# Grouped FFNs with two sends in flight and a longer clear, softmax rows divided before they are turned, late routing split

## The chip, the cores and the metric

The kernel runs on one core of a Trainium2 chip. The metric is the device time of one execution in microseconds (us). A core has five engines with an instruction stream each: TensorE (PE in the profile; PEld is its weight loading), VectorE (DVE), ScalarE (ACT), GpSimd (POOL) and SyncE (SP), and DMA queues that move data between on-chip memory and the chip's main memory. SP's and POOL's instruction streams issue the transfers that matter here: SP plain ones, POOL the indirect ones, in which every partition of a tile goes to, or comes from, a row whose number stands in an index tile.

## The reference

The program is a "macaron" of two layers on x of 8 x 512 x 256 fp32, which are 4096 tokens of 256 columns:

```python
x = x + 0.5 * _L0_ffn_ref(_layernorm(x), ...)    # 8 experts that choose their tokens
x = x + _L0_attn_ref(_layernorm(x), ...)         # rope, causal, 16 heads of 16
x = x + 0.5 * _L0_ffn_ref(_layernorm(x), ...)
x = x + 0.5 * _L1_ffn_ref(_layernorm(x), ...)    # 16 experts, grouped routing, top 4
x = x + _L1_attn_ref(_layernorm(x), ...)         # 16 heads of 64, returns x + z
x = x + 0.5 * _L1_ffn_ref(_layernorm(x), ...)
```

The last three lines are those that the change touches. In the grouped FFN every token gets a softmax over 16 experts; the best two of four groups stay, and of their experts the best four are taken, with the softmax values as weights:

```python
g = scores.reshape(T, N_GROUPS, N_EXPERTS // N_GROUPS)
_, gidx = lax.top_k(g.max(axis=-1), TOPK_GROUPS)
...
masked = (g * gmask[..., None]).reshape(T, N_EXPERTS)
_, indices = lax.top_k(masked, TOPK)
weights = jnp.take_along_axis(original_scores, indices, axis=1)
...
a = jax.nn.silu(h1) * h3
y = jnp.einsum('tei,eid,te->td', a, w2, c)
z = jax.nn.silu(xt @ ws1) * (xt @ ws3) @ ws2
return (y + z).reshape(shape)
```

Expert width is 128, the shared expert's 256. In the second attention

```python
scores = jnp.einsum('bhqk,bhmk->bhqm', q, k) * scale
weights = jax.nn.softmax(scores, axis=-1)
z = jnp.einsum('bhqm,bhmk->bhqk', weights, v)
```

with q, k and v from three projections of the normalized x, and z times `w_o` added to x.

## The kernel before

The 4096 tokens are 32 token tiles of 128 (TT = 32), four of them (QT = 4) to a sequence of 512 (CH). x stays in on-chip memory throughout. `tile_kernel` (L2392) runs `ffn0`, `attn0`, `ffn0`, then `ffn1_before` (L2149, the first grouped FFN, class `Grouped`), `attn1` (L1029) and `ffn1_after` (L2297, the last grouped FFN, class `Joint`, a subclass of `Grouped`). From L2149 on the order of the instructions on every engine is the one written in the code.

**A grouped FFN.** The tokens are cut into two parts (12 and 20 tiles in the first, `PARTS`; 20 and 12 in the last, `LAST`). For each part, `logits` on PE, then `routing` on DVE (with a few products on PE) gives every token four slot numbers, sorted by expert (`slot`), and four weights (`coef`). `send` (L1488, in `Joint` L1844 on) issues four indirect DMAs for each token tile on POOL, which write the tile's normalized rows to their slots in main memory (`slots_d`). A send waits until an earlier send has landed: in `Grouped` the one three before it (`self.sent[-3:-2]`, the third last of those issued), in `Joint` the one two before it. Behind the four sends `Grouped.send` lets POOL clear `self.pause`, 128 x 512. `tile_steps` then runs over the slots in steps of two tiles of 128 rows: SP loads `xs`, PE transposes (`turn`, `tpx`), multiplies by w1 and w3 of the tile's expert (`hide`, `hs`), transposes (`back`, `tpa`) and multiplies by w2 (`give`, `yps`); the stages of four successive steps are interleaved, and SP stores `ys` to `ys_d`. The loads of a part wait for all sends of the part. Evictions from PSUM go to ACT or DVE by the parity of the step (`evict`). Last, `gather` on POOL fetches the four rows of each token from `ys_d` into `yg`, with a clear behind each four, and `add` on DVE adds them, weighted, to x.

In `ffn1_before` the shared expert's products fill PE while the routing and the sends of part 0 run. The gathers of part 1 come in `attn1`, whose code also prepares part 0 of the last FFN: means and roots of the layer norm, normalized rows on POOL (L1484), transposes and logits (`Front`), its routing (`routing`, one piece at a time, from chunk NC * groups + 7 = 47 on) and its 80 sends. `ffn1_after` loads the expert weights on SP (for each group of four experts w1, w3 and w2, all 512 columns wide or less), runs the first three steps of part 0, normalizes the last four token tiles, computes their logits, routes all 12 tiles of part 1 on DVE while PE goes on with part 0, and sends them as soon as the slots are there. The gathers begin at step `known + 3`, and the rest of them is spread over the shared expert's units.

**The second attention.** A chunk is one sequence and two heads: 64 chunks (N), 8 (NC) to a sequence, each in two halves of two query tiles. The loop at L1281 goes through half-steps g. Half-step g holds: the turning of the first of the two query tiles of half-step g - 1 (`turn`: 4 transposes for each head into `tp`, evicted to `eT` by ACT for the first head, DVE for the second), a piece of side work (`pieces`), the projection to q (evicted by ACT) or k (by DVE) of the next chunk (`side`), the turning of the second query tile, the scores of this half-step (`scores`: 4 products into `sp`, DVE takes the negated maximum of each query tile, ACT the exponentials with their sums into `ex`), and a filling (`fill`) that PE does while DVE and ACT work: in half 0 the products of the weights with v of the chunk before (`products`, `zp`), in half 1 projections of the sequence before (`project`) or columns and values of the next.

The exponentials are turned as they are. The division by the row sums comes behind the products: `reciprocals` takes 1/sums of a chunk (DVE), and ACT spreads them to `wide`, 128 x 512; `spread` turns `wide` on PE (4 transposes into `rp`), ACT copies the result to `rs`; `scale` multiplies `zp` by `rs` on DVE into `zn`. All PSUM tiles named `tp`, `rp`, `pq`, `pv`, `yp`, `row` share one tag of three buffers ("m").

`roots` computes the layer norm's 1/sqrt in two pieces with a square root on ACT (`ln_root`) and Newton steps on DVE (`ln_rest`); `ln_guess` (L195) does the same on DVE alone, from integer operations and three Newton steps.

Of the kernel before, what the change touches and what calls it, by code (L numbers as in the profile page):

```python
# [19 lines left out]
P = 128  # L20
# [49 lines left out]
class Kernel:  # L70
# [124 lines left out]
    def ln_guess(self, pool, stats, t0, n):  # L195

# [11 lines left out]
        for i in range(3):  # L208
# [5 lines left out]
            y = new  # L214

# [820 lines left out]
    def _attn1(self, ctx, weights, one, after):  # L1036
# [61 lines left out]
        def scores(n, half):  # L1098
# [4 lines left out]
            sps = []  # L1103
# [9 lines left out]
            for i, sp in enumerate(sps):  # L1113
# [3 lines left out]
                ex = ch["ex", qt] = work.tile([P, 2, CH], F32, name="ex", bufs=4)  # L1117
                for j in range(2):
                    nc.scalar.activation(  # L1119
                        ex[:, j, :], sp[:, j, :], AF.Exp,  # L1120
                        bias=nmax[:, j : j + 1], accum_out=ch["sums"][:, qt, j : j + 1],
                    )

# [9 lines left out]
        def reciprocals(n):  # L1133
            ch = chunk[n]
            rec = work.tile([P, QT, 2], F32, name="rec", bufs=2)
            nc.vector.reciprocal(rec, ch["sums"])
            ch["wide"] = work.tile([P, QT, 2, DK1], F32, name="wide", bufs=1)
            nc.scalar.copy(ch["wide"], bc(rec, 3, DK1))

        def spread(n):  # L1140
            ch = chunk[n]
            rp = bank("rp")
            for qt in range(QT):
                nc.tensor.transpose(  # L1144
                    rp[:, qt * P : qt * P + P], ch["wide"][:, qt].rearrange("p h d -> p (h d)"), self.ident
                )
            ch["rs"] = work.tile([P, CH], F32, name="rs", bufs=1)
            nc.scalar.copy(ch["rs"], rp)
# [13 lines left out]
        def scale(n):  # L1162
            zn = work.tile([P, CH], F32, name="zn", bufs=11)
            nc.vector.tensor_tensor(zn, chunk[n]["zp"], chunk[n]["rs"], ALU.mult)
# [29 lines left out]
        def roots(ranges):  # L1194
            ys = []

            def first():
                for stats, t0, n in ranges:
                    ys.append(self.ln_root(pool, stats, t0, n))

            def second():
                for (stats, t0, n), y in zip(ranges, ys):
                    self.ln_rest(pool, stats, t0, n, y)
            return [first, second]
# [75 lines left out]
        side(0, 1)  # L1280
        for g in range(2 * N + 1):  # L1281
# [3 lines left out]
            if half == 0 and n < N:  # L1285
                todo += listed(n)
            if half == 1 and n > 0:
                scale(n - 1)
            if g > 0:
                turn(m, 2 * mh, 0)  # L1290
                turn(m, 2 * mh, 1)
            if half == 0 and n > 0:
                reciprocals(n - 1)
            pieces(1)
            if n + 1 < N:
                side(n + 1, half)
# [3 lines left out]
            if half == 0 and n > 0:  # L1300
                spread(n - 1)
            if n < N:
                scores(n, half)
# [8 lines left out]
                for piece in fill(n, half):  # L1312
                    piece()
            else:
                products(n - 1)
        scale(N - 1)
# [4 lines left out]
        for i in range(QT):  # L1321
            project(B - 1, i)
            self.ln_mean(self.late, after.stats, (B - 1) * QT + i)

# [137 lines left out]
class Grouped:  # L1462
# [25 lines left out]
    def send(self, h, t, row):  # L1488
# [3 lines left out]
        for r in range(TOPK):  # L1492
# [6 lines left out]
            before = self.sent[-3:-2]  # L1499
# [157 lines left out]
    def expert_weights(self, groups=range(4)):  # L1657
        nc, w = self.k.nc, self.k.w
        for g in groups:
            es = slice(g * 4, g * 4 + 4)  # L1660
            nc.sync.dma_start(
                out=self.w13[:, es, :, 0:INTER], in_=w["w1"][es].rearrange("e (c p) i -> p e c i", p=P)
            )
            nc.sync.dma_start(
                out=self.w13[:, es, :, INTER:], in_=w["w3"][es].rearrange("e (c p) i -> p e c i", p=P)
            )
            nc.sync.dma_start(out=self.w2[:, es], in_=w["w2"][es].rearrange("e p d -> p e d"))
# [821 lines left out]
```

## Time and profile before

| what | us |
|---|---|
| three runs, median (lowest to highest) | 3820.96 (3817.65 to 3825.62) |
| profiled execution, its time | 3822.71 |
| its span in the profile | 3821.0 |
| `ffn0`, `attn0`, `ffn0` | 0 to about 1741 |
| `ffn1_before` | 1741 to 2168 |
| `attn1`, with its last projections | 2168 to 3409 |
| `ffn1_after` | 3409 to 3821 |
| PE busy in 2168 to 3391 | 1212.0 of 1223 |
| DVE, ACT, POOL busy there | 749.2, 645.0, 240.0 |
| PE busy in 3409 to 3620 | 179.9 of 211 |
| PE busy in 3620 to 3821 | 170.7 of 201; POOL 151.4 |

The stages are told apart by the lines of their instructions. A group of the profile is one line of code, one engine and one form of operation, with its count, its busy time in us, the mean in ns of one, and behind the second bar the time that the engine stood idle just ahead of it and what it then waited for. An arrow in a timeline's brackets gives the idle time before an instruction and its releaser. The granted clock of PE over the span is 0.968 of full speed.

The two largest groups of the second attention show its shape:

```profile
L1119 ACT ACTIVATE ex<-sp,nmax 128x512 f32<-128x512 f32 x512 | 345.1, 686 | 238.8 <-DVE nmax L1116 238.7
...
L1116 DVE TENSOR_REDUCE nmax<-sp 128x2 f32<-128x1024 f32 x256 | 301.6, 1220 | 81.4 <-PE sp L1110 81.4
```

### The profile page before, as it was taken

How to read it: one execution, taken by the hardware profiler on the slowest of the kernel's cores; microseconds unless marked ns; L12 is line 12 of the kernel's file. 1: busy time of each engine (PE TensorE's matmuls, PEld its weight loads, DVE VectorE, ACT ScalarE, POOL GpSimd, SP SyncE). 2: the span in 40 equal slices, each digit the busy share in tenths (PEclk: the TensorE clock that was granted, in tenths of full speed). 3: DMA queues.
4: the chain of work that ended last, by engine and by line, in shares of the span. 5: the costliest groups of instructions: out<-in, count | busy, mean ns of one | idle time of the engine just before them, and what ended most of it. 6: DMA issues, size and time to landing. Idle time of an engine off the chain costs nothing.

```text
span 3821.0 us, 51805 instructions
## 1 busy us (share of the span) xinstructions
PE 3583.2 (94%) x18293; PEld 2235.2 (58%) x18293; DVE 1860.9 (49%) x4500; ACT 1451.8 (38%) x2922; POOL 1244.2 (33%) x1142
## 2 busy tenths in 40 slices
PE   4999999999996899998989999999999999988988
PEld 1566664555553566666678745555555555557865
DVE  6212205665655312116535566666556567546355
ACT  3222223444444222221123355555555555532321
POOL 2333235343331333333763312220000002714177
PEclk7999999999998899998999999999999999999989
DMA  5355442000113233324467401000000000135564
GB/s 194 97 139 146 109 103 85 23 18 23 29 34 96 49 69 78 71 41 134 135 219 236 135 18 31 28 26 1 1 1 1 1 1 23 72 113 185 163 182 130
DMA packets 258173, 309.32 MB, mean 81 GB/s; under 512 B 34048, under 2 KB 227968, under 8 KB 257664
## 3 DMA queue, kind: packets, MB, share of 16 engines
q1 hardware_dynamic: 182144, 177.78, 14.8%
q0 software_dynamic: 49152, 101.24, 10.7%
q10 hardware_dynamic: 26624, 27.00, 2.1%
q8 instruction: 151, 2.47, 0.3%
q14 instruction: 102, 0.84, 0.1%
HBM read 159.51 MB, written 138.02 MB: 78 GB/s over the span
## 4 chain that ended last, share of the span: by engine, by line
PE 37%; issue 8%; POOL 6%; DMA 2%; DVE 1%; ACT 0%; POOLq 0%; DVEq 0%; SPq 0%; ACTq 0%
PE sp L1110 6%; PE tp L1130 6%; PE pq L1088 6%; PE zp L1157 6%; PE pv L1077 3%; PE yp L1172 3%; POOL slots_d L1493 3%; PE hs L1786 2%; POOL yg L2010 2%; PE hs L2073 1%; PE yps L1808 1%; POOL slots_d L1857 1%; PE rp L1144 1%; DMA yg<-ys_d,slot 1%; PE yps L2095 1%
## 5 line engine op out<-in xcount | busy, mean ns | idle before, releaser
L521 PE MATMUL hp<-exT,w 128*128 128x512 f32 x1024 | 453.4, 597 | 0.7 <-DVE exT L509 0.7
L552 PE MATMUL op<-w,hid 128*128 128x256 f32 x2048 | 451.9, 379 | 0.0
L1119 ACT ACTIVATE ex<-sp,nmax 128x512 f32<-128x512 f32 x512 | 345.1, 686 | 238.8 <-DVE nmax L1116 238.7
L552 PEld LDWEIGHTS op<-w,hid 128*128 128x128 f32 x2048 | 386.8, 190 | 64.1 <-issue 14.4
L557 DVE TENSOR_TENSOR ob<-op,b 128x256 f32<-128x256 f32 x128 | 54.4, 425 | 642.8 <-PE op L552 555.3
L1116 DVE TENSOR_REDUCE nmax<-sp 128x2 f32<-128x1024 f32 x256 | 301.6, 1220 | 81.4 <-PE sp L1110 81.4
L531 POOL DMA_INDIRECT acc_d<-ob,idx x128 | 201.7, 1576 | 419.3 <-ACT ob L558 353.2
L812 DVE CUSTOM_DVE_ANT_0 junk<-sp,mask 128x128 bf16<-128x128 f32 (+3 forms) x512 | 251.2, 491 | 166.4 <-PE sp L803 142.3
L521 PEld LDWEIGHTS hp<-exT,w 128*128 128x128 f32 x1024 | 192.8, 191 | 221.5 <-issue 216.7
L1130 PEld LDWEIGHTS tp<-ident,ex 128*128 128x128 f32 x2048 | 233.8, 141 | 144.7 <-issue 84.7
L525 ACT ACTIVATE hid<-hp,b 128x512 f32<-128x512 f32 x256 | 175.9, 687 | 317.0 <-PE hp L521 317.0
L1130 PE MATMUL tp<-ident,ex 128*128 128x128 f32 x2048 | 272.9, 275 | 6.6 <-ACT ex L1119 4.1
L1110 PE MATMUL sp<-qk,qk 64*128 64x512 f32 x1024 | 254.4, 615 | 0.0
L1601 POOL DMA_INDIRECT yg<-ys_d,slot x128 | 129.6, 1013 | 359.2 <-DVE x L1614 267.0
L1088 PE MATMUL pq<-xnT,wide 128*128 128x512 f32 x512 | 244.1, 600 | 1.2 <-ACT xnT L250 0.8
L252 DVE COPY eT<-tp 128x512 f32<-128x512 f32 x256 | 177.1, 692 | 138.7 <-PE tp L1130 138.5
L1157 PE MATMUL zp<-eT,v 128*64 128x512 f32 x1024 | 234.0, 598 | 0.0
L250 ACT COPY eT<-tp 128x512 f32<-128x512 f32 x256 | 149.8, 585 | 220.1 <-PE tp L1130 220.1
L492 POOL DMA_INDIRECT ex<-xn_d,idx x128 | 131.5, 1027 | 297.8 <-DVE idx L483 263.6
L558 ACT ACTIVATE ob<-ob,gate 128x256 f32<-128x256 f32 x128 | 65.0, 508 | 413.9 <-DVE ob L557 413.9
L1059 POOL TENSOR_TENSOR x<-x,xn 128x1024 f32<-128x1024 f32 x8 | 18.9, 2360 | 544.1 <-DVE xn L1054 544.1
L855 ACT ACTIVATE ex<-st 128x1024 f32<-128x1024 f32 x160 | 155.1, 1022 | 95.1 <-PE st L848 95.1
(432 smaller groups left out, 6024.6 us busy)
## 6 DMA issues: line engine op xcount, KB each, us to landing
xs<-slots_d SPq DMA_DIRECT2D x149, 256.0 KB, 2.9
ys_d<-ys SPq DMA_DIRECT2D x149, 256.0 KB, 2.9
w<-in_W SPq DMA_DIRECT2D x32, 1024.0 KB, 5.2
slots_d<-zero ACTq DMA_DIRECT2D x7, 2304.0 KB, 12.8
w_sb<-in_w SPq DMA_DIRECT2D x24, 512.0 KB, 7.6
xn_d<-xn SPq DMA_DIRECT2D x16, 512.0 KB, 3.1
acc_d<-x SPq DMA_DIRECT2D x16, 512.0 KB, 4.4
x<-acc_d SPq DMA_DIRECT2D x16, 512.0 KB, 7.0
```

Source lines behind the costliest of these rows:

```text
L252: self.nc.vector.tensor_copy(out, in_)
L521: nc.tensor.matmul(hp, lhsT=w1[:, c, f * P : f * P + P], rhs=exT[e][:, c, h * CH : h * CH + CH], start=(c == 0), stop=(c == DC - 1),)
L525: nc.scalar.activation(hid[h][:, f, :], hp, AF.Gelu, bias=b1[:, e, f : f + 1])
L531: inst = nc.gpsimd.indirect_dma_start(out=acc_d[:, :], out_offset=bass.IndirectOffsetOnAxis(ap=idx[:, e, st : st + 1], axis=0), in_=ob, in ...
L552: nc.tensor.matmul(op, lhsT=hid[h][:, f, i * P : i * P + P], rhs=w2[:, f, :], start=(f == 0), stop=(f == FC - 1),)
L812: nc.vector.tensor_tensor_reduce(out=junk[:, :wd], in0=sps[h // 2][:, h % 2, at : at + wd], in1=mask[:, S - wd :], scale=1.0, scalar=NEG, ...
L1088: nc.tensor.matmul(pp, lhsT=(wq, wk)[a][:, k, c * P : c * P + P], rhs=xnT[b][:, k, :], start=(k == 0), stop=(k == DC - 1),)
L1110: nc.tensor.matmul(sp[:, j, :], lhsT=q[r, qt * P : qt * P + P], rhs=k[r, :], start=True, stop=True)
L1116: nc.vector.tensor_reduce(nmax, sp, AX.X, ALU.max, negate=True)
L1119: nc.scalar.activation(ex[:, j, :], sp[:, j, :], AF.Exp, bias=nmax[:, j : j + 1], accum_out=ch["sums"][:, qt, j : j + 1],)
L1130: nc.tensor.transpose(tp[:, k, :], ch["ex", qt][:, j, k * P : k * P + P], self.ident)
L1157: nc.tensor.matmul(zp[DK1 * j : DK1 * j + DK1, :], lhsT=v[b, h][:, k, at : at + DK1], rhs=ch["eT"][:, j, k, :], start=(k == 0), stop=(k == ...
```

## The change

**Sends of the first grouped FFN.** A send waits for the one two before it; the clear behind each four is 128 x 1024.

**The second attention.** `reciprocals` and `spread` are gone. `divide`, new, takes the reciprocals of one query tile's two sums on DVE and scales the two heads' exponentials in place before they are turned: on DVE, or, where `shared` holds, the first head on ACT. `shared` holds for chunks up to parts[1] + 2 = 22, in which the gathers and sums of the first FFN run, and from chunk 47 until part 0 of the last FFN is routed. The division of the first query tile stands behind its exponentials and ahead of the second's, that of the second behind the half-step's filling. `scale` becomes a copy on ACT. Where the filling of the half-step before was empty, `side` comes ahead of the first turning. `roots` uses `ln_guesses`, the pieces of `ln_guess`.

**Routing of the last FFN's second part.** `routing` is split: `choose` is what depends on a token tile alone (softmax, groups, top four). Two `choose` of four tiles each run in `attn1`, the first from half-step 2 * (N - NC) + 4 on as 13 pieces of two advances, the second behind the last half-step; what they find is kept in a `yg` buffer (`kept`). `ffn1_after` chooses for the last four tiles only and then goes on with all 12. `Cut` gives tiles of the full size and returns their first columns.

**Weights and order of the last FFN.** The host lays w1 and w3 together in the order of the on-chip tile, and w2 too. SP issues w13 of three groups, four loads of `xs`, w13 of the fourth group, w2 in two halves, the shared weights. Two steps, the root and the normalized rows, the third step, then columns and logits. `lean` sends the evictions of the steps to ACT while the routing runs. Two of the `normal`s move between the sends. In `Joint`, sends of part 1 have a clear of 1024 columns behind each four. The gathers start at `known + 5`, and in the shared part three half-tokens come to four units.

```diff
--- before.py
+++ after.py
...
-        def scores(n, half):
+        def scores(n, half, shared):
...
-            sps = []
+            sps, exps = [], []
...
+                exps.append((qt, sp, nmax, ex))
+            for qt, sp, nmax, ex in exps:
                 for j in range(2):
                     nc.scalar.activation(
                         ex[:, j, :], sp[:, j, :], AF.Exp,
                         bias=nmax[:, j : j + 1], accum_out=ch["sums"][:, qt, j : j + 1],
                     )
+                if qt == 2 * half:
+                    divide(n, qt, shared)
...
+        def divide(n, qt, shared):
             ch = chunk[n]
...
+            rec = work.tile([P, 2], F32, name="rec", bufs=4)
+            nc.vector.reciprocal(rec, ch["sums"][:, qt])
+            ex = ch["ex", qt]
+            for j in range(2):
+                if shared and j == 0:
+                    nc.scalar.mul(ex[:, j, :], ex[:, j, :], rec[:, j : j + 1])
+                else:
+                    nc.vector.tensor_scalar(ex[:, j, :], ex[:, j, :], rec[:, j : j + 1], None, ALU.mult)
...
-            nc.vector.tensor_tensor(zn, chunk[n]["zp"], chunk[n]["rs"], ALU.mult)
+            nc.scalar.copy(zn, chunk[n]["zp"])
...
+            guesses = [self.ln_guesses(pool, stats, t0, n) for stats, t0, n in ranges]
+            return [lambda g=g: next(g, None) for g in guesses for _ in range(3)]
...
+            if g == 2 * (N - NC) + 4:
+                after.kept()
+                early = [
+                    after.choose(
+                        after.lg1[:, t : t + QT], Cut(front.pool, a), after.score1[:, t : t + QT], after.hots1[:, :, t : t + QT]
+                    )
+                    for t in (0, QT)
+                ]
+                todo += [each(advance, early[0], 2)] * 13
...
-            if g > 0:
-                turn(m, 2 * mh, 0)
-                turn(m, 2 * mh, 1)
-            if half == 0 and n > 0:
-                reciprocals(n - 1)
-            pieces(1)
-            if n + 1 < N:
-                side(n + 1, half)
+            for one_of in ("side", "turn") if not filled else ("turn", "side"):
+                if one_of == "turn" and g > 0:
+                    turn(m, 2 * mh, 0)
+                    turn(m, 2 * mh, 1)
+                    pieces(1)
+                if one_of == "side" and n + 1 < N:
+                    side(n + 1, half)
...
-            if half == 0 and n > 0:
-                spread(n - 1)
             if n < N:
-                scores(n, half)
+                shared = n <= one.parts[1] + 2 or n >= NC * groups + 7 and not flags["routed"]
+                scores(n, half, shared)
...
+                filler = fill(n, half)
+                for piece in filler:
                     piece()
+                filled = bool(filler)
+                divide(n, 2 * half + 1, shared)
...
+        advance(early[1], 11)
         scale(N - 1)
...
+            advance(early[1], 6)
...
-            before = self.sent[-3:-2]
+            before = self.sent[-2:-1]
...
-    def expert_weights(self, groups=range(4)):
+    def expert_weights(self, groups=range(4), back=True):
...
+            nc.sync.dma_start(out=self.w13[:, es], in_=w["w13"][:, es])
+            if back:
+                nc.sync.dma_start(out=self.w2[:, es], in_=w["w2"][:, es])
+
+    def back_weights(self):
+        nc, w = self.k.nc, self.k.w
+        for h in range(2):
+            es = slice(h * 8, h * 8 + 8)
+            nc.sync.dma_start(out=self.w2[:, es], in_=w["w2"][:, es])
...
+        if h == 1:
+            nc.gpsimd.memset(self.pause, 0.0)
...
+        yield from self.choose(
+            lg[:, chosen:], Cut(pool, HT), score[:, chosen:], hots[:, :, chosen:]
+        )
...
-            k.evict(st[j]["aT"][:, :n], tp[:, :n, :P], j)
+            k.evict(st[j]["aT"][:, :n], tp[:, :n, :P], j | self.lean)
...
-        f.pause = k.late.tile([P, TOPK, D], F32, name="yg", bufs=2).rearrange("p r d -> p (r d)")[:, :CH]
+        f.pause = k.late.tile([P, TOPK, D], F32, name="yg", bufs=2)
...
-        f.expert_weights(range(1))
+        f.expert_weights(range(3), False)
         for j in range(4):
             load(j)
-        f.expert_weights(range(1, 4))
+        f.expert_weights(range(3, 4), False)
+        f.back_weights()
         f.shared_weights()
         g = TT // QT - 1
-        for i in range(3):
+        for i in range(2):
             step(i)
         k.ln_guess(f.route, f.stats, g * QT, QT)
         f.normal(g)
+        step(2)
         f.columns(g)
...
+        f.lean = 1
+        steps = f.routing(1, f.lg1, f.route, f.row_psum, f.parts[1] - QT)
+        advance(steps, 1)
...
-        begin, at, ends = known + 3, 0, 2 * (len(order) + 3)
+        begin, at, ends = known + 5, 0, 2 * (len(order) + 3)
...
-                sending = not advance(steps, 4)
-                if i < 2:
-                    f.normal(rest.pop(0))
+                sending = not advance(steps, 6 if i < 7 else 3)
                 if sending:
+                    f.lean = 0
+                    fill = f.route.tile([P, 2 * CH], F32, name="pause")
+                    f.pause = fill
+                    tokens = list(range(f.parts[1]))
+                    for t in tokens[-QT:] + tokens[:-QT]:
+                        if t % QT == 0 and t < tokens[-QT]:
+                            f.normal((a + t) // QT)
+                            rest.remove((a + t) // QT)
                         f.send(1, t, f.xn[:, a + t, :])
...
-            while at < ends and (at - from_) * units < (ends - from_) * done_units:
+            units += 1
+            if at < ends and 4 * (at - from_) < 3 * units:
                 fetched(at)
```

## The prediction

> **What bounds the kernel now.** I read the page first (busy shares, slices, chain of waits), then the engines' busy time by stage, then the lines of each changed stage, then the timeline around PE's few gaps.
>
> ```profile
> PE 3583.2 (94%) x18293; PEld 2235.2 (58%) x18293; DVE 1860.9 (49%) x4500; ACT 1451.8 (38%) x2922; POOL 1244.2 (33%) x1142
> ...
> PE   4999999999996899998989999999999999988988
> ```
>
> PE is the bound nearly everywhere; the dents are the three changed stages' seams. By stage (columns: window, its length, then busy time and count of PE, weight loads, DVE, ACT, POOL, then granted clock, DMA share, GB/s):
>
> ```profile
> 1888.00:1985.00 97.00, 97.00 (x536) 86.16 (x537) 35.66 (x73) 32.03 (x73) 74.62 (x84) 1.00 0.72 230
> 1985.00:1994.00 9.00, 0.65 (x5) 0.34 (x4) 0.00 (x0) 0.65 (x2) 4.03 (x5) 0.80 0.37 118
> 2168.00:3391.00 1223.00, 1211.99 (x5781) 653.62 (x5780) 749.23 (x1179) 644.96 (x1518) 239.95 (x216) 1.00 0.05 18
> ```
>
> The second attention (row 3) is PE from end to end: 1212 of 1223 us; DVE has 474 us free, ACT 578. The first grouped FFN stops PE once (row 2), at the seam between its token parts:
>
> ```profile
> 1985.16 0.38 PE L1800 MATMUL tpa<-ident,as 128*128 128x128 f32 x2
> 1993.90 1.11 PE L1772 MATMUL tpx<-ident,xs 128*128 128x128 f32 x4 [8.35 <-DMA xs<-slots_d]
> ```
>
> PE steps arrive every 3.25 us until part 0 is used up; part 1's rows are read only after all its sends have landed (last send issued 1988.42). So these sends already end PE's wait. The same seam in the last FFN, and the routing ahead of it:
>
> ```profile
> 3465.48 1.05 POOL L1857 DMA_INDIRECT slots_d<-wide,slot  x1 [98.10 <-DVE slot L1979]
> ```
>
> ```profile
> 3552.88 1.11 PE L2058 MATMUL tpx<-ident,xs 128*128 128x128 f32 x4 [7.16 <-DMA xs<-slots_d]
> ```
>
> ```profile
> 3622.21 1.06 POOL L2010 DMA_INDIRECT yg<-ys_d,slot  x1 [73.63 <-DMA ys_d<-ys]
> ```
>
> Slots at 3465.5 start 48 sends; they end at 3547.6; PE, out of part 0 at 3545.7, resumes 7.2 us later; the first gather waits for outputs of part 1's steps; 128 gathers then occupy POOL to 3814.8, and 6 us later the span ends.
>
> **A. Sends of the first grouped FFN.** Now: four sends at 1.29 us spacing (0.98 + 0.30 issue) and a clear of 512 columns (0.54):
>
> ```profile
> L1506 POOL MEMSET yg<- 128x512 f32 x32 | 17.4, 543 | 0.0
> L1857 POOL DMA_INDIRECT slots_d<-wide,slot x48 | 47.0, 979 | 134.2 <-DVE slot L1979 98.1 <-DMA slots_d<-wide,slot 32.5 <-issue 3.7
> ```
>
> The second row is the same send with two in flight: 48 sends from 3465.5 to 3547.6, 47 spacings of 1.75 us, 32.5 us of it waiting for landings. The clear of 1024 columns is not in the trace; doubling 0.543 gives 1.08, bounded by 0.54 (all fixed cost) and 1.09 (none). Landing takes 3.1 us in 1888–1990 (DMA 72% busy), 2.4 when quieter. With 3.3 us between a send and the second after it, and 2.1 us where the clear stands, one group of four spaces 2.1 + 1.29 + 2.01 + 1.29 = 6.7; by the late stage's 1.75 it is 7.0, and 7.25 if the clear hides poorly. I take 7.0 under load and 6.4 when quiet, against 5.57 and 5.83 now. Part 0: 12 groups from 1803.35 end at 1880 instead of 1872; PE is in the shared expert until 1885.5, which hides it. Part 1: 20 groups from 1880: 15.2 by 1987 (107/7.0), where PE runs dry; 4.8 × 6.4 = 31 more, to 2018. The last send issues 2.1 us before that; landing and load take 5.5 as now (1988.42 to 1993.90), so PE resumes near 2021 instead of 1993.9: **+27**. Ends: +14 (6.4 throughout, part 1 pulled to 2008) and +45 (7.7, the late spacing plus most of the clear). Nothing behind takes it back, since attention is PE-bound; what is late next is the gathers in attention, whose POOL is busy 240 of 1223.
>
> **B. Second attention: rows divided before they are turned.** Off PE: four transposes per chunk of two heads.
>
> ```profile
> L1144 PE MATMUL rp<-ident,wide 128*128 128x128 f32 x256 | 40.9, 282 | 2.0 <-DVE eT L252 1.8 <-ACT wide L1138 0.2
> L1138 ACT COPY wide<-rec 128x512 f32<-128x512 f32 x64 | 39.6, 619 | 39.4 <-DVE rec L1136 37.8 <-DVE y L191 1.4
> L1148 ACT COPY rs<-rp 128x512 f32<-128x512 f32 x64 | 37.5, 586 | 21.5 <-PE rp L1144 21.5
> L1164 DVE TENSOR_TENSOR zn<-zp,rs 128x512 f32<-128x512 f32 x64 | 44.2, 690 | 79.9 <-PE zp L1157 79.8
> ```
>
> Start to start in the timeline (2492.44 to the scores at 2493.01) they hold PE 0.57 us: 64 × 0.57 = **−36.5**. Some 4 us of PE's 11 idle should go as well (the turns' waits on exponentials next to table loads; the side work now comes first behind an empty fill).
>
> Added per chunk: four reciprocals (0.16 by the smallest DVE rows) and eight scalings of 128x512. On DVE: one-pointer rows of 128x256 take 354 and 347 ns, small ones 0.19, so 0.16 more per 256 columns: about 0.5; I take 0.48. Bounds 0.39 (from 287 ns at 256) and 0.75 (twice-pointered rows take 406 to 470 at 256, full rate). On ACT: 128x256 with a pointer is 508 ns (the gate scaling); 512 columns more cost 335 ns (1022 at 1024 columns less 687 at 512), so 256 more make 0.68; I take 0.70, with 0.69 (the exponentials) and 1.02 (twice 508) as ends. A count of the condition: chunks 0–22 and 47–54 are shared (31; first head on ACT), 33 are not: 264 + 124 = 388 scalings on DVE, 124 on ACT. DVE becomes 749 + 388 × 0.48 + 256 × 0.16 − 44 − 12 + 33 (C, D) = 953 of 1186 (80%); ACT about 670 (57%). So no engine displaces PE on the mean; the place matters.
>
> The order within a half-step: count from the end of its scores. Maxima end at 0.44 (the second 1.2 us tile), exponentials run from 0.55 in four of 0.69 plus readout; the first row tile is complete at 2.03, the second at 3.36. PE fills 3.58 us (products or projections), turns the first tile at 3.58, does q or k, turns the second at 6.2. Unshared: reciprocal to 2.25, scalings to 2.76 and 3.24, needed 3.58 and 4.0: slack 0.3 to 0.8. Shared: behind exponentials, scalings and two evictions in ACT's order the third turn's PSUM bank comes free at 6.4–6.55 and is wanted at 6.23: 0.2–0.4 us late in 31 steps, some 9; with 3 for a late DVE eviction after value fills, **+12**. The added wait stands on ACT ahead of the next exponentials and on DVE ahead of evictions; PE waits for both. Sum of B: −36.5 − 4 + 12.5 = **−28**. Ends: −42 (no stall) and −5 (0.28 per half-step over 128).
>
> The POOL rows beside DVE work: sends average 1018 ns in attention against 979 in the last FFN, so little contention is seen. The Trainium skill, "SBUF — State Buffer", section "SBUF: two separate sides", speaks against this change: a DVE operation in a two-port mode takes the port pair shared with GpSimd for its whole length, and descriptors for POOL's DMAs then can't be written; it gives about 620 ns growing to 3100. No run here shows such a scaling beside sends; by that rule each of 216 POOL instructions could wait one scaling (0.48 us, some 104 us of POOL, which has 980 free), so the sum would move little unless DVE waits for POOL instead.
>
> **C. Guesses for the layer-norm roots.** 18 table loads of 1283 ns leave ACT; PE waited about 2 us on them (in the 4 above). DVE gets some 13 us of small operations, hidden.
>
> **D to G. The last FFN.** Early routing of eight tiles goes to DVE in attention's last chunks (30 pieces; DVE has 0.4 of each step free there): 0, and if uncovered up to +10. The rest of the routing works on 64 instead of 192 columns (0.22 against 0.355 us an operation, two dozen of them, with four fewer normals before it): the stretch from logits to slots shrinks from 33.9 to about 25 us. Logits come near 3422 instead of 3431.4: the third step goes after the normal, and the 7.1 us for weights (first wait of the stage on `w_sb`) shrink as the first halves arrive first in larger runs. Evictions on ACT while routing remove the 10.3 us that PE waits on DVE's `aT`. Sends then start near 3447.6, 18 us sooner. The clear behind each four (7.0–7.25 a group, 85 us for 12) ends them near 3532, PE resumes near 3537 against 3552.9: −16. Gathers move with it: 32 groups at 5.68 are 182 of their 192.5 us, so POOL holds the end. Start two steps later and three quarters of a half-token per unit may cost 1: **−15**, ends −22 (all stalls gone) and 0 (POOL's gathers end where they did).
>
> **Sum** on the span of 3821.0: 27 − 28 − 15 = −16, so 3805; the profiled execution took 3822.71 (1.7 around the span), 1.75 above the median 3820.96, and so the same step from the median gives 3805.
>
> **Rivals.**
> 1. *The division becomes attention's bound* (slower). Between exponentials and turn there are 128 half-steps; each costs s. Total: 27 − 40.5 + 128 s − 15, zero at s = 0.22 us, +0.2% at 0.28. With s = 0.4 (scalings at 0.75, or ACT's chain late in every step): +23, **3844**. For: 0.3 us of slack is thin, and PE's turns already wait only on exponentials. Against: 20% of DVE free, unshared timetable closes.
> 2. *Sends cost little* (landing quick at lower load, clear hidden): A = +6, sum −37, **3784**. For: waits were only 8 us in 107. Against: the late stage's 1.75.
> 3. *The last FFN gives nothing*: gathers pace the end whatever starts them, and B gives −24: 27 − 24 − 3 = 0, **3821**. For: POOL is busy 151 of 193 there. Against: the first gather waits for outputs, which come sooner.
>
> **Numbers.** Forecast 0.43 (3790–3815), rival 1 0.27, rival 2 0.11, rival 3 0.19. A measurement tells 0.2% (7.6 us) from no change. Faster: forecast 0.42, rival 2 0.11, one in 0.53; same: rival 3 with the edges, 0.20; slower 0.27. The range 3778–3843 leaves out deep cases of rivals 1 and 2, about 0.2.
>
> **What would show it.** Right: no `rp` group; PE's wait before `tpx` at the seam 30–38 us instead of 8.35; scalings of 128x512 near 480 ns; PE idle in attention near 20; first late send 38 us after the last projection. Wrong: `tp` waiting on DVE `ex` for over 30 us (rival 1), the seam under 20 us (rival 2), the first late gather still 213 us after the last projection (rival 3). What would make it wrong altogether: a scaling at 0.75 or POOL stalling DVE.

## The result and the profile after

The changed kernel takes 3832.18 us (median of six runs, 3831.61 to 3842.13) where the kernel before takes 3823.48 (six runs, 3817.65 to 3825.62). The ratio is 1.003, with a 95% interval of 1.002 to 1.004: slower by about 0.3%, where 3805 was forecast. The profiled execution of the changed kernel took 3831.61 with a span of 3829.9, against 3822.71 and 3821.0 before. Of all the executions reported below one, in the first experiment, ran at a granted clock of 0.82 and took 4325 us; the ratio there leaves it out.

The head of the page, engines' busy time and PE's row of the slices:

```profile
span 3829.9 us, 51745 instructions
...
PE 3553.5 (93%) x18037; PEld 2202.8 (58%) x18037; DVE 2045.0 (53%) x5170; ACT 1479.4 (39%) x2966; POOL 1276.8 (33%) x1154
...
PE   4999999999996899998968999999999999989886
```

PE is busy 30 us less than before and the program is 9 us longer, so PE waits 39 us more. The waits are placed by cutting both profiles at the same instructions: the first transpose of the second attention, the end of its last projection, the end of the program.

| stretch | before | after | difference | forecast |
|---|---|---|---|---|
| start to attention's first transpose | 2166.4 | 2191.3 | +24.9 | +27 |
| second attention | 1242.9 | 1238.8 | -4.0 | -28 |
| last FFN | 411.8 | 399.8 | -12.0 | -15 |
| span | 3821.0 | 3829.9 | +8.9 | -16 |

The timeline of the changed kernel at the three places shown before (the seam of the first FFN, the first late send, the seam of the last FFN and the first late gather):

```profile
2016.87 1.12 PE L1782 MATMUL tpx<-ident,xs 128*128 128x128 f32 x4 [35.14 <-DMA xs<-slots_d]
```

```profile
3468.26 1.05 POOL L1867 DMA_INDIRECT slots_d<-wide,slot  x1 [76.50 <-DVE past L2014]
```

```profile
3555.49 1.11 PE L2087 MATMUL tpx<-ident,xs 128*128 128x128 f32 x4 [9.87 <-DMA xs<-slots_d]
```

```profile
3626.18 1.08 POOL L2039 DMA_INDIRECT yg<-ys_d,slot  x1 [74.16 <-DMA ys_d<-ys]
```

The wait at the first seam has grown from 8.35 to 35.14 us. Counted from the last projection (3430.1 now, 3409.2 before), the first late send comes at 38 instead of 56 us, the seam at 125 instead of 144, the first gather at 196 instead of 213. By stage (window, length, busy time and count of PE, weight loads, DVE, ACT, POOL, then clock, DMA share, GB/s):

```profile
1985.00:2018.00 33.00, 1.12 (x4) 0.72 (x4) 0.40 (x1) 0.00 (x0) 22.83 (x24) 0.50 0.29 98
2191.00:3430.00 1239.00, 1217.52 (x5614) 644.04 (x5614) 943.00 (x1873) 667.19 (x1553) 247.32 (x216) 0.99 0.07 24
```

In attention DVE is busy 943 us and ACT 667, almost what was worked out (953 and 670), and PE idles 21 us instead of 11. The new groups:

```profile
L1151 DVE TENSOR_SCALAR ex<-ex,rec 128x512 f32<-128x512 f32 x386 | 190.4, 522 | 9.0
L1149 ACT ACTIVATE ex<-ex,rec 128x512 f32<-128x512 f32 x126 | 91.4, 725 | 35.8 <-DVE rec L1145 35.7
L1514 POOL MEMSET yg<- 128x1024 f32 x32 | 31.0, 970 | 0.0
```

### The profile page after: what moved, and what is told of

Its sections match the earlier page's. It is cut to its first block, busy times and chain, and to the rows that moved or that the text cites. A ratio compares the mean times of both kernels' runs of the same rounds, so it can differ in the third digit from the quotient of the medians.

```text
span 3829.9 us, 51745 instructions
## 1 busy us (share of the span) xinstructions
PE 3553.5 (93%) x18037; PEld 2202.8 (58%) x18037; DVE 2045.0 (53%) x5170; ACT 1479.4 (39%) x2966; POOL 1276.8 (33%) x1154
## 3 DMA queue, kind: packets, MB, share of 16 engines
q1 hardware_dynamic: 163296, 177.77, 14.4%
## 4 chain that ended last, share of the span: by engine, by line
PE 35%; POOL 5%; issue 5%; DVE 4%; DMA 3%; ACT 2%; POOLq 0%; SPq 0%; DVEq 0%; ACTq 0%
PE sp L1115 5%; PE tp L1139 5%; PE pq L1093 5%; PE zp L1160 4%; POOL slots_d L1501 3%; PE hs L2102 2%; PE pv L1082 2%; PE hs L1796 2%; PE yp L1175 2%; PE hp L1718 1%; ACT ex L1126 1%; PE yps L2124 1%; PE yps L1818 1%; DVE ex L1151 1%; DVE nmax L1121 1%
## 5 line engine op out<-in xcount | busy, mean ns | idle before, releaser
L1151 DVE TENSOR_SCALAR ex<-ex,rec 128x512 f32<-128x512 f32 x386 | 190.4, 522 | 9.0
```

Source lines behind the costliest of these rows:

```text
L1151: nc.vector.tensor_scalar(ex[:, j, :], ex[:, j, :], rec[:, j : j + 1], None, ALU.mult)
```

## The experiments

Twelve kernels ran, in three groups of four, each group on one chip beside the kernel before. Neither of the two chips they fell on (the first and the third group on one) treated the kernel before as the result's executions had done: there it took 3924, 3902 and 3920 us. "The first chip" below is that of the result. No later run of the kernel before came near 3823, so whether the chip or the time makes the difference is not shown. Experiments are therefore compared by the stretches of their profiles and, within a group, by their times.

**Three in flight and the short clear in the changed kernel.**

```diff
-            before = self.sent[-2:-1]
+            before = self.sent[-3:-2]
...
-        f.pause = k.late.tile([P, TOPK, D], F32, name="yg", bufs=2)
+        f.pause = k.late.tile([P, TOPK, D], F32, name="yg", bufs=2).rearrange("p r d -> p (r d)")[:, :CH]
```

> The changed kernel with three sends in flight again in the first grouped FFN and the short clear of 512 columns. Theory S (the seam): PE's wait before the first rows of part 1 falls from 35.1 us to about 8, and nothing behind it takes that back, since attention and the last FFN start as much earlier: 3832 - 25 = 3807 us, 0.4% faster than the kernel before. Rival (the seam's time is swallowed later, for instance by gathers that start sooner and meet attention's first steps): 3815 to 3825.

Measured 3912.17 us (3881 to 3919, and the one of 4325) beside 3924.03: ratio 0.996 (0.994 to 0.998). Attention began at 2242.4, not at 2166. Theory S is neither shown nor refuted by this run: something else had stretched the first FFN, in both kernels with three in flight and the short clear.

**The sends alone, on the kernel before** (the same two lines the other way round).

> The kernel before with only the sends changed: two in flight and the clear of 1024 columns in the first grouped FFN. Theory S: slower by 25 us, 3823 + 25 = 3848, with a wait of PE of about 35 us at the seam. Rival (part of the 25 us comes from other parts of the change, such as the larger weight transfers): less than 15 us, 3838 or below.

Measured 3862.60 (3859 to 3872): 61 us faster than the kernel before beside it, 0.984 (0.981 to 0.986). The seam is as theory S has it, 35.10 us of waiting, and attention begins at 2204.5 (2191.3 in the result; 9 of these 13 us stand already before the first send). What makes this a gain there is that the kernel before loses some 80 us in the same stretch on this chip.

**No division.**

```diff
-            rec = work.tile([P, 2], F32, name="rec", bufs=4)
-            nc.vector.reciprocal(rec, ch["sums"][:, qt])
...
-                    nc.scalar.mul(ex[:, j, :], ex[:, j, :], rec[:, j : j + 1])
-                else:
-                    nc.vector.tensor_scalar(ex[:, j, :], ex[:, j, :], rec[:, j : j + 1], None, ALU.mult)
```

> The changed kernel without any reciprocal or scaling in the second attention, so that its weights are not normalized: PE does the same work, DVE loses 386 scalings and 256 reciprocals, ACT 126 scalings. Theory P (the place of the division costs some 20 us of PE in steps where a scaling is late, with the lower clock that follows a wait): attention shortens by 15 to 20 us, 3832 - 18 = 3814. Rival R (these stalls are the routing's and the new order's own): it shortens by less than 6 us, above 3826. The spread through PE was worth 0.48 us a chunk, 31 us in all, so attention from first transpose to last projection should come to 1243 - 31 = 1212 if nothing else stalls.

Measured 3822.65. Attention takes 1207.4 us: 35.5 less than before and 31.4 less than in the changed kernel. The whole kernel is only 9.5 us faster than the 3832 of the result, because the last FFN took 416.9 us in this profile instead of 399.8. POOL waits 26.5 us there for sums; why is not shown, and the program without the division computes other values. Attention's row:

```profile
2191.00:3399.00 1208.00, 1200.89 (x5615) 641.85 (x5615) 734.78 (x1232) 583.45 (x1428) 240.91 (x216) 1.00 0.07 24
```

PE's matmuls are those of the changed kernel. It idles 7.1 us where the changed kernel idled 21.5, and is busy 16.6 us less on the same matmuls (1200.9 instead of 1217.5). PE's longest sums of waits in attention (in all, times, longest), first the changed kernel repeated below, then without the division:

```profile
PE tp L1139 <- DVE ex L1151: 7.1, 9, 2.7
PE tp L1139 <- DVE eT L257: 2.1, 6, 0.5
PE tp L1139 <- DVE rank L1349: 1.9, 1, 1.9
PE tp L1139 <- ACT ex L1149: 1.9, 1, 1.9
PE tp L1139 <- DVE v L1086: 1.6, 3, 0.9
```

```profile
PE tp L1139 <- ACT qk L1099: 2.2, 3, 1.0
PE tp L1139 <- ACT ex L1126: 1.5, 2, 1.3
```

The turns wait for scalings and for evictions that stand behind scalings. The one wait put down to a routing operation (`rank`) is of this kind too: in the result's profile eight routing operations, with a pause for ACT among them, fill DVE's order from 3094.6 to 3099.0; the scaling runs behind them to 3099.6, an eviction to 3100.2, `rank` to 3100.35. Theory P stands: the order and the routing cost little without the division, and the division where it stands costs attention 31 us. Three other profiles with the changed attention (the first experiment, the repetition and the old pace below) have 1231.1 to 1231.4 us, so there it is 24. Both are more than P had.

**The long clear alone, on the kernel before.**

> The kernel before with the clear of 1024 columns alone, three sends in flight. By the changed kernel's row the longer clear takes 0.97 us instead of 0.54, so a group of four goes from 5.83 to 6.3 where no landing is waited for: 20 groups of part 1 and the end of part 0 that PE does not cover give 8 to 14 us at the seam, 3823 + 11 = 3834. If the clear lies inside waits for landings it costs under 4 us; if the clear is the whole of the 25 us, 3848.

Measured 3848.77 (3836 to 3854) beside 3924.03. There is no long wait at its seam, but the tile steps ahead of it are slow (below), so the price of the clear by itself can't be read from it. Attention begins at 2177.5, 70 us sooner than in the kernel before on this chip (2247.3, below): with three in flight, the longer clear alone takes most of that loss away.

**The changed kernel again.**

> The changed kernel once more, beside the kernel before on one chip. In the first four runs the kernel before took 3924 us and the changed kernel with three sends in flight 3912, while the kernel before with two in flight and the long clear took 3863. Theory C (three indirect stores in flight hold up the other transfers of the first grouped FFN in some runs or on some chips, and two don't): the changed kernel stays at 3830 to 3850 wherever it runs, and the kernel before lies at 3820 or at 3920. Rival (those runs were disturbed as a whole): both move together.

Measured 3830.90 beside 3902.04: 0.983 (0.980 to 0.986). Theory C: the changed kernel keeps its time, the kernel before doesn't. Its attention took 1231.4 us, 7 less than in the first profile, with nearly the same waits:

```profile
2199.00:3431.00 1232.00, 1211.15 (x5614) 641.56 (x5614) 943.55 (x1875) 665.34 (x1553) 247.60 (x216) 1.00 0.07 24
```

PE idles 20.9 us (21.5 there) and is busy 6.4 us less on the same matmuls. By the traces' records of the clock, 20.5 us of attention ran at a granted clock of 0.50 in the result's profile, 6.8 us here, and none without the division.

**The old pace of the last gathers.**

```diff
-        units, from_ = 0, at
+        units, done_units, from_ = len(pump.units), 0, at
...
-            units += 1
-            if at < ends and 4 * (at - from_) < 3 * units:
+            done_units += 1
+            while at < ends and (at - from_) * units < (ends - from_) * done_units:
```

> The changed kernel with the old spread of the last gathers and sums over the shared expert's units (by share of the units done, instead of three half-tokens to four units). In the changed kernel POOL waits 9.3 us in seven times for sums that free the gather buffers, all behind the 90th of 128 gathers; before there was 0.3 us of this. Theory G (the new pace is too slow near the end): this wait goes and the time falls by 5 to 7 us against the changed kernel run beside it. Rival (the end is held by something else behind the sums): no more than 2 us.

Measured 3824.52, 6.4 below the changed kernel beside it. In the profiles 6.0 us of this are seen: the last FFN went from 397.4 to 394.0, and 2.5 us lie ahead of attention, where the edit changes nothing. So the pace is worth some 3.5 us. POOL's waits in the last FFN, with the new pace (the repetition), then with the old:

```profile
POOL yg L2039 <- DMA yg<-ys_d,slot: 9.9, 13, 1.6
POOL yg L2039 <- DVE x L1622: 6.8, 3, 4.5
```

```profile
POOL yg L2039 <- DVE x L1622: 6.9, 5, 3.5
POOL yg L2039 <- DMA yg<-ys_d,slot: 2.6, 4, 1.0
```

The wait for sums, which theory G said would go, stays; what went is a wait for earlier gathers. Theory G is right in sign and not in its mechanism.

**The late choice back in the last FFN** (the early `choose` left out of attention, `routing` choosing for twelve tiles).

> The changed kernel with the choice of experts for all twelve late token tiles back in the last FFN. Theory: attention loses some 2 to 3 us of waits in chunks 58 to 62, and the sends of the last FFN start later, by the 7 to 9 us that choosing for 192 instead of 64 columns takes, so it is 4 to 7 us slower than the changed kernel. Rival (early choice costs attention as much as it brings): within 2 us.

Measured 3836.25, 5.3 slower. Half-steps 116 to 120 take 36.3 instead of 37.6 us, so early choice costs attention 1.3 there, though attention as a whole took 1233.8 us, 2.5 more than with it; sends start at 40.8 instead of 35.5, gathers at 199.8 instead of 193.6. Moving the choice pays.

**Short holds.**

```diff
-                nc.gpsimd.tensor_tensor(self.x[:, ts, :], self.x[:, ts, :], xn[b], ALU.add)
+                for i in range(QT):
+                    t = b * QT + i
+                    nc.gpsimd.tensor_tensor(self.x[:, t, :], self.x[:, t, :], xn[b][:, i, :], ALU.add)
```

> The changed kernel with POOL's eight additions of 128x1024 to x in the second attention cut into four of 128x256 each. In the changed kernel six DVE scalings that start while such an addition runs take 1.6 to 2.6 us instead of 0.49 and end with it. Theory L (one engine's instruction keeps the other from the memory port until it ends): none of the scalings takes over 1.2 us, and the half-steps 52, 68 and 84 lose their 0.9 us each, about 3 to 5 us in all. Rival (DVE waits for something that POOL's addition only accompanies, or takes turns with all four pieces): the scalings stay as long and the time within 1 us.

In the changed kernel, on POOL and DVE at once (start, length, instruction):

```profile
2693.71 2.36 POOL L1064 TENSOR_TENSOR x<-x,xn 128x1024 f32<-128x1024 f32 x1 [92.90 <-DVE rec L1145]
2693.73 3.02 DVE L1151 TENSOR_SCALAR ex<-ex,rec 128x512 f32<-128x512 f32 x2
```

Two scalings that take 0.88 us elsewhere take 3.02: the first ends 0.28 us behind POOL's addition. With short additions (count, then shortest, median and longest in ns), first the changed kernel, then this one:

```profile
L1151 DVE TENSOR_SCALAR ex<-ex,rec x386: 467/486/2620, 2204.5 to 3409.4; 128x512 f32<-128x512 f32 x193
```

```profile
L1153 DVE TENSOR_SCALAR ex<-ex,rec x386: 468/486/949, 2212.8 to 3406.8; 128x512 f32<-128x512 f32 x193
```

The longest scaling falls from 2620 to 949 ns, attention from 1231.4 to 1227.2. The six half-steps with such a scaling are 0.70 or 0.90 us shorter each, 4.8 in all, here and in both later runs with short additions: theory L. The time does not follow (3834.44, one run of four at 3822.43), because the last FFN took 407.9 us in this profile; there POOL waits 21.5 us for sums, for a reason that is not shown.

**The kernel before once more, profiled.**

> The kernel before itself, profiled where it runs now. On the first chip it took 3823 us, on two others 3924 and 3902, while the changed kernel took 3832 and 3831. Theory C: the 80 to 100 us are all in the first grouped FFN while sends and tile steps run together (from about 1885 to the last send): there PE waits step after step for rows or for the stores' buffers, as it does in the changed kernel with three in flight and the short clear (its attention began at 2242 instead of 2191); attention and the last FFN keep their 1243 and 412 us. Rival: the loss is spread over all transfers, attention and last FFN included. On a chip where it doesn't occur the time is 3820 to 3830.

Measured 3922.05 beside 3919.69. Attention begins at 2247.3 (2166.4 on the first chip) and takes 1242.9 as there; the last FFN takes 421.7 instead of 411.8. So 81 us of the loss come ahead of attention and 10 behind it. The same 80 us of the first FFN, with tile steps and sends together, on the first chip and here:

```profile
1905.00:1985.00 80.00, 80.00 (x443) 71.09 (x442) 30.21 (x62) 26.85 (x61) 61.78 (x70) 1.00 0.72 231
```

```profile
1905.00:1985.00 80.00, 37.89 (x145) 28.52 (x143) 8.95 (x18) 7.59 (x17) 63.39 (x71) 0.68 0.41 135
```

POOL issues its sends as fast in both (56 and 57), but the second has done 8 tile steps (activations `sgs`) where the first has done 24. ACT's groups there, with what ended the idle time:

```profile
L1792 ACT ACTIVATE sgs<-hs 128x256 f32<-128x256 f32 x8 | 3.1, 383 | 37.9 <-remote 30.3 <-PE tpx L1772 3.1 <-issue 2.2
```

Taken in order, the eight activations start 1.16, 0.04, 0.04, 0.35, 5.85, 12.45, 21.21 and 35.18 us behind their products (0.04 in all 24 on the first chip). "Remote" says that the profile doesn't know the releaser, so what holds the engines up stays open. That two sends in flight end it, the next run shows.

**Two in flight and the short clear, on the kernel before.**

> The kernel before with two sends in flight and its short clear of 512 columns. If the number in flight is what holds the other transfers up, this is as fast as with the long clear or faster: 3845 to 3865 on a chip where the kernel before takes 3900 or more, about 3840 where it takes 3823. If it is the pause that POOL's queue gets behind each four, it stays near the kernel before there, above 3880; three in flight with the long clear came out at 3849 beside 3924.

Measured 3859.13 (3858 to 3861) beside 3919.69. The hold-up is gone (23 activations in the same 80 us, 0.04 us behind their products):

```profile
1905.00:1985.00 80.00, 75.80 (x420) 67.12 (x418) 27.93 (x57) 25.63 (x59) 52.20 (x58) 1.00 0.64 207
```

PE is busy for 75.8 of the 80 us, POOL does less, and the wait at the seam is 32.65 us, against 34.1 to 36.9 in the profiles with two in flight and the long clear. So two in flight end the hold-up and make nearly the whole seam; the clear adds 1.5 to 4.3 us to the wait. Three in flight are not enough for the loss of 80 us, though: with the long clear most of it was gone too.

**Both mends, two in flight**, and **with three in flight and the long clear.**

> The changed kernel with the old pace of the last gathers and POOL's additions in attention cut in four. By the runs so far the pace is worth 4 to 6 us and the cut 4 us of attention: 3831 - 9 = 3822. If the last FFN's end wanders as it did with the cut alone (408 us instead of 397), 3828.

> As the kernel with both mends, but with three sends in flight in the first grouped FFN and the long clear kept. With the long clear alone on the kernel before, the seam had cost only a few us where two in flight cost 35: 3822 - 13 = 3809, which would beat the changed kernel and, on every chip so far, the kernel before. If three in flight bring the hold-up back, above 3830.

Measured 3825.90 (3815 to 3842) and 3809.78 (3806 to 3816) beside 3919.69. The first, forecast at 3822, is too spread to be told from the changed kernel. The second is 16 us below the first, with attention beginning at 2176.1 instead of 2192.3, and 0.973 (0.968 to 0.977) of the kernel before. It is below every run of the two kernels on any of the chips, 0.4% below the kernel before on the first one, though it didn't run there. Some hold-up is left in it, as the same stretch shows (19 activations instead of 24):

```profile
1905.00:1985.00 80.00, 66.99 (x345) 54.56 (x342) 23.11 (x47) 21.03 (x48) 65.48 (x67) 1.00 0.66 214
```

PE is busy for 67 of the 80 us, between the 80 of the first chip and the 38 above.

## Why the prediction was wrong

The forecast missed by 24.9 us: 24.0 in attention, 3.0 in the last FFN, and -2.1 at the seam.

**A, the seam: right.** +27 was forecast and +24.9 came. A group of four took 7.1 us up to 1985 (7.0 taken) and 6.1 behind it (6.4), the clear 0.97 us (1.08), the last send went out at 2011.4 and PE resumed at 2016.9 (2021 forecast). That it agrees within 2 us is in part luck: the first send went out at 1797.9 instead of 1803.4, in code that the change doesn't touch, and over all profiles it lies between 1797.7 and 1807.0. The clear was priced as part of the spacing. With two in flight and the short clear a group took 7.1 us up to 1985 and 5.7 behind it: beside the tile steps the clear is almost free, and while PE stands still it costs its whole 0.43 us a group.

**B, attention: this is the step that failed.** It read -36.5 for the spread, -4 for idle time, +12.5 for stalls. Without the division attention gained 35.5, against the 40.5 of the first two terms: the turns of `rp` held the scores up by 0.48 us a chunk (half-steps of 9.66 became 9.19), not the 0.57 between two starts, so 31 instead of 36.5; the idle time was as forecast. The third term was mis-sized: +12.5 became 31.4 in the profile of the result and 24.0 in the repetition. As idle time it was nearly right: PE idles 14.4 us more with the division than without it (13.7 in the repetition). What the term left out is that PE is also busy 16.6 us longer (10.3) on the same matmuls. At half speed the 20.5 us (6.8) with a granted clock of 0.50 are worth at most 10.2 (3.4) of that, an estimate; the rest, 6 to 7 us in both, is not explained. So the signs of being right all came (no `rp`, a seam of 35.1 us, scalings of 486 ns, PE idle 21 us, the first late send at 38 us), and the forecast was wrong: none of them looks at how long PE's own work takes.

The term was also put in the wrong place. "The third turn's PSUM bank" being 0.2 to 0.4 us late in 31 steps hardly occurs: half-steps 9 to 23, all shared, lose 1.0 us together. What is lost, by the half-steps of the repetition less those without division:

| half-steps | lost, us | what is late |
|---|---|---|
| 0 to 9 | 3.9 | the division behind value fills; one short fill at half-step 7 |
| 9 to 46 | 2.3 | two holds by POOL's additions (0.7 each), small waits |
| 48 to 88 | 4.7 | three holds by POOL (0.9 each); DVE's sums of projections ahead of it |
| 88 to 110 | 7.4 | DVE's routing operations ahead of the scaling; one hold by POOL (0.7) |
| 116 to 126 | 3.9 | early choice; half-steps without filling |

These are 22 of the 24 us; the rest lies in the first and last projections.

The timetable was made for a half-step in which DVE had only the attention's work, and the share of 80% busy was taken as room. But the division stands in DVE's order, behind single operations of 0.5 to 1.5 us and behind whole runs of them (4.4 us of routing at half-step 94); the slack worked out was 0.3 to 0.8. Some of the waits are then paid twice, where PE's clock falls. In the changed kernel's timeline at half-step 7:

```profile
2263.22 1.88 PE L1093 MATMUL pq<-xnT,wide 128*128 128x512 f32 x4
...
2270.86 1.09 PE L1139 MATMUL tp<-ident,ex 128*128 128x128 f32 x8 [1.89 <-ACT ex L1149]
2272.68 3.78 PE L1093 MATMUL pq<-xnT,wide 128*128 128x512 f32 x4 [0.72 <-ACT xnT L255]
```

After 1.89 and 0.72 us of waiting the same four products take 3.78 instead of 1.88 us, at a granted clock of 0.50. Rival 1 is the nearest: by its formula, with the 35.5 measured, s is 31.4 / 128 = 0.25 us instead of the 0.4 that it was priced at. But it had scalings at 0.75 us or a late step everywhere, and its sign, turns waiting over 30 us on DVE's `ex`, did not come (7.5 us, in 9 waits): most half-steps lose nothing, thirteen lose 0.7 to 2.5 us each.

**The rule on the shared port.** By the Trainium skill, "SBUF — State Buffer", section "SBUF: two separate sides", an operation of DVE in a two-port mode and one of GpSimd keep each other out for the whole instruction. The prediction set it aside "unless DVE waits for POOL instead". It does: six scalings of 386 end within 0.3 us behind POOL's 2.36 us additions, worth 4.8 us of attention by the half-steps that short additions made shorter. The sends were hardly slowed: 1050 ns on the mean against 1018.

**C, the roots: right,** hidden as forecast, in the 4 us of idle time; of 18 table loads in attention one is left.

**D to G, the last FFN: right in kind,** -12.0 for -15. The sends began 38.1 us behind the last projection (38.4 forecast), PE resumed at 125 (128), the gathers began at 196 (197). The term that was off is the time of the gathers: 1 us was taken; the 128 gathers took 198.6 us instead of 192.5. In this profile POOL waits for sums (`x`) that free the gather buffers near the end. Its waits in the last FFN, after and before:

```profile
POOL yg L2039 <- DMA yg<-ys_d,slot: 9.3, 14, 1.5
POOL yg L2039 <- DVE x L1622: 9.3, 7, 4.5
```

```profile
POOL yg L2010 <- DMA yg<-ys_d,slot: 9.1, 10, 2.1
...
POOL yg L2010 <- DVE x L1614: 0.3, 1, 0.3
```

The waits for earlier gathers are the same; those for sums are new here. That the new pace makes them is not shown: with the old pace they stayed, and the kernel before, as it is and with two in flight, waits 9.5 and 10.9 us for sums on the other chip, with the old pace. With it the gathers took 194.3 us, 4.4 less than in the repetition.

**What was not in the prediction at all** is that three sends in flight, with the short clear, can cost 80 us. Nothing in the profile of before shows it, and on the chip of the result it didn't occur. On the one other chip where both kernels ran side by side, the same change is a gain of 1.7% (ratio 0.983).

## What to carry to other kernels

When work is moved from the bounding engine to one that is 60% busy, the share says that it fits, not when it runs: write down the longest operation, or run of operations, that can stand ahead of it in that engine's order and compare it with the slack, step by step, in every stage that shares the engine. And count what a wait does to the bounding engine's own work, not only the idle time. A price taken between two starts overstates what removing the instruction gives; look for a step with it and one without. And a setting of transfers in flight should be tried at more than one time and on more than one chip before its price is believed.

## What was not expected of the hardware

One and the same program took 3823 us with the result and 3902 to 3924 on the two chips of the experiments, 81 of 91 us (in the one profile of it there) where three indirect stores were in flight beside tile steps; on that chip it took 3859 and 3863 with two in flight, and 3849 with three and the clear of 1024 columns. The activations' distance from their product grew from 0.04 to as much as 35 us while the stores' own spacing didn't change (5.7 us a group of four, 5.9 on the first chip).

A single wait of PE of 1.9 us was enough for a granted clock of 0.50 from 2271.9 on, for 6.8 us, with a wait of 0.7 in them. The same two waits in the repetition were followed by 3.4 us at 0.50. The Trainium skill, "TensorE: Matmul & The Clock Gate", section "What's actually happening", has the clock fall after an idle window of about 3.4 us; here less idle time did it, and the measurement decides.
